# A grouped 3x3 convolution as 32x32 products on 16 tiles of the array, with its operand copies spread over five engines

## The chip, the cores and the metric

The kernel runs on one core of a Trainium2 chip. The metric is device time in microseconds (us) of one execution. A core has a matrix engine (TensorE, PE in the profile; its weight loads are shown as PEld), VectorE (DVE), ScalarE (ACT), GpSimd (POOL) and SyncE (SP), which issues transfers. Each engine keeps its own program order, and they meet at semaphores. Transfers run on 16 DMA engines. Tensors live in SBUF, 128 partitions wide; products are summed in PSUM, which has eight banks of 512 float32 numbers in each partition.

## What is computed

The input is `x`, 8 images of 128 channels and 56 x 56 pixels, float32. Four layers follow each other, each of the form `x = x + layer(group_norm(x))`, the norm being over 32 groups of four channels of one image:

- layer 0: attention between windows of 8 x 8 pixels, with a depthwise 3x3 convolution;
- layer 1: a batch norm, a projection, and a recurrence of 512 units over all pixels in order, then a projection back;
- layer 2: the layer that is changed, below;
- layer 3: two 3x3 convolutions with batch norms and a residual.

Layer 2 in the reference, with `O = I = 128` and `p = 4`:

```python
i = jnp.arange(O)[:, None]
j = jnp.arange(I)[None, :]
m3 = (j - i) % p == 0
w3m = w3 * m3[:, :, None, None].astype(w3.dtype)
out = conv_general_dilated(x, w3m, window_strides=(1, 1), padding=((1, 1), (1, 1)))
w1m = w1 * (~m3).astype(w1.dtype)
out = out + jnp.einsum('oi,bihw->bohw', w1m, x)
out = out + b.sum(axis=1)[None, :, None, None]
```

So the channels fall into four classes of 32 (by their number modulo 4). Within a class there is a 3x3 convolution of 32 x 32 channels; between different classes there is a 1x1 convolution. The kernel keeps channels sorted by class, one class in each quarter of 32 partitions.

## The kernel before

All eight images stay in SBUF as `X`, 128 partitions by 8 x 3136 pixels. An image is cut into seven blocks of 8 rows (448 pixels; `NBLK = 7`), 56 blocks in all, and a block's sum takes one PSUM bank.

**Layer 2** (in `convolutions`). `Norm` makes an image's statistics on VectorE (`bn_stats` per block, then an aggregate), spreads them over the four channels of a group with two small products on PE (`mean_mm`, `var_mm`), takes a root on ScalarE, and then writes the normalised image with a border of zeros into one of two buffers `pads` (L1314, VectorE). `spread` (L1318 to L1333) builds `g3`: for every class, its 32 channels three times, in three quarters of the partitions, moved by 0, 1 and 2 pixels. Of the twelve pieces of each chunk of rows, three are copies by ScalarE (L1331) and nine are transfers, issued by SP or by GpSimd (L1333). `within` (L1343) does a block's taps: for each of three filter rows and each class one product with 96 rows of weights and 32 columns, so that the four classes use four column tiles of the array. `between` (L1351) adds the 1x1 convolution as one 128x128 product, two blocks at a time. `add` (L1358) adds the sum and the bias to `X` on VectorE, and `stats3` (L1421) makes the statistics for layer 3.

The order of PE, ScalarE, VectorE and GpSimd is the order in which the loop over the 56 blocks writes the instructions (`manual_schedule`): in block `n` of image `b` the loop does the taps, then small steps of the next image's norm, then the adds, then the next image's `normal` and `spread`. Transfers issued by SP are in the order of the program too. Layer 2 starts when layer 1's last outputs are in `X`; before its first product, image 0 must have been normalised and spread. Products that only keep PE at work (`warm`, L897) fill that time.

**Layer 1.** The recurrence runs over 17 stretches of pixels at once, two pixels per turn of the loop. Within the second part of its turns, VectorE takes statistics (`stats`, L984, `bn_stats` over 32 pixels of 16 stretches) of image 0 as its pixels become final; the last two pieces come after the loop. The other images' statistics are made in layer 2 (L1281).

**Layer 3** starts with image 0, whose normalised rows and transforms (`normal3`, `all_sums`) are made while layer 2 does its last image. `tail` and `late` are the last images' statistics, which are finished inside layer 3. `outputs` uses three scratch tiles `s`, `d` and `w`.

## Time and profile before

| | us |
|---|---|
| median of 3 executions | 3253.57 (3253.45 to 3254.02) |
| the profiled execution | 3253.89, its span 3251.9 |
| PE busy | 3178.3 (98%) |
| VectorE busy | 2270.8 (70%) |
| ScalarE busy | 1270.3 (39%) |
| GpSimd busy | 1475.3 (45%) |
| layer 1's recurrence ends, layer 2's first product | 2640, 2653.5 |
| layer 3's first product | 2844.6 |

The profile is of one execution. A line of a group names the line of the kernel, the engine, the operation, what it writes and reads, how often, the busy time and the mean duration of one in ns, and then how long the engine was idle ahead of such instructions and what ended that. Each float32 product appears as two records of PE and two of PEld. Matmuls are pipelined, so their busy times overlap, and starts tell more than durations. Times in a timeline are from the start of the span.

### The profile page before, as it was taken

To read this page: it belongs to the slowest core of one execution; us is meant where nothing else is said; L and a number is where in the kernel's file an instruction comes from. 1 tells how busy PE (TensorE), PEld (TensorE's weight loads), DVE (VectorE), ACT (ScalarE), POOL (GpSimd) and SP (SyncE) were. 2 spreads that over 40 slices of the span, in tenths; PEclk is the share of its full clock that TensorE was granted. 3 is DMA by queue.
4 is the path that set the end of the run, shared out by engine and by line. 5 is a ranking of instruction groups with operands and counts; after the bars stand their busy time and mean duration, and the time that the engine had idled before them with its cause. 6 is when DMAs were issued, how large, how long until landed. Compare 5 with 4: busy or idle time off the path is not lost.

```text
span 3251.9 us, 104559 instructions
## 1 busy us (share of the span) xinstructions
PE 3178.3 (98%) x40784; PEld 2679.8 (82%) x40784; DVE 2270.8 (70%) x5756; ACT 1270.3 (39%) x2425; POOL 1475.3 (45%) x4147
## 2 busy tenths in 40 slices
PE   8999999999999989999999999999999999999998
PEld 5767677676766679999999999999999973399998
DVE  5888888888887866666555555555532347799998
ACT  4555555555555532221111111111111244556564
POOL 4888888888777843333222222222200036522221
PEclk8999999999999999999999999999999999999999
DMA  5555555555455421110000000000022236500001
GB/s 156 135 143 131 143 137 138 142 135 143 120 137 145 121 63 49 49 49 29 1 1 1 1 1 1 1 1 1 8 58 61 59 104 166 144 16 36 31 36 46
DMA packets 188167, 239.09 MB, mean 74 GB/s; under 512 B 42848, under 2 KB 137568, under 8 KB 187664
## 3 DMA queue, kind: packets, MB, share of 16 engines
q0 software_dynamic: 40896, 123.47, 14.0%
q1 hardware_dynamic: 130256, 101.95, 10.9%
q10 hardware_dynamic: 16512, 6.90, 0.9%
q8 instruction: 324, 5.31, 0.7%
q14 instruction: 179, 1.47, 0.2%
HBM read 133.64 MB, written 67.56 MB: 62 GB/s over the span
## 4 chain that ended last, share of the span: by engine, by line
PE 83%; DVE 10%; issue 2%; POOL 2%; ACT 1%; DMA 1%; ACTq 0%; POOLq 0%; DVEq 0%; SPq 0%
PE ps L1086 27%; PE q L1051 9%; PE po L1116 5%; PE s L539 5%; PE po L605 5%; PE pc L1343 4%; PE t L581 4%; PE plep L420 4%; PE pc3a L1663 3%; PE pc3b L1663 3%; PE pi L1021 3%; DVE nmax L546 2%; PE t L571 2%; PE pc L1351 1%; PE py L446 1%
## 5 line engine op out<-in xcount | busy, mean ns | idle before, releaser
L1086 PE MATMUL ps<-hs,w_gates 128*128 128x136 f32 x7680 | 928.8, 279 | 0.0
L1086 PEld LDWEIGHTS ps<-hs,w_gates 128*128 128x128 f32 x7680 | 911.6, 190 | 4.5
L1100 ACT ACTIVATE hs<-v 128x272 f32<-128x272 f32 x538 | 212.3, 404 | 1167.3 <-DVE v L1098 1167.3
L546 DVE TENSOR_REDUCE nmax<-s 128x2 f32<-128x512 f32 x784 | 486.3, 684 | 169.3 <-PE s L539 167.6
L591 ACT ACTIVATE e<-t 128x512 f32<-128x512 f32 x784 | 429.5, 596 | 339.8 <-PE t L581 261.8
L1098 DVE TENSOR_TENSOR v<-ps,g 128x272 f32<-128x272 f32 x538 | 216.3, 411 | 494.6 <-PE ps L1086 407.3
L1039 POOL TENSOR_TENSOR d<-inp 128x136 f32<-128x136 f32 x186 | 87.8, 472 | 789.1 <-DVE inp L1027 789.1
L498 POOL COPY ks<-kT 128x64 f32 x1568 | 297.2, 235 | 120.6 <-PE t L581 69.0
L605 PE MATMUL po<-e,ring 128*32 128x64 f32 x12544 | 244.9, 230 | 6.1 <-DVE nmax L546 5.5
L605 PEld LDWEIGHTS po<-e,ring 128*32 128x32 f32 x12544 | 217.9, 149 | 31.0 <-DVE nmax L546 7.9
L581 PE MATMUL t<-qm,ks 32*128 32x128 f32 x6272 | 237.3, 273 | 1.3 <-issue 1.3
L539 PE MATMUL s<-ks,qm 32*128 32x256 f32 x3136 | 233.9, 403 | 4.4 <-ACT vp L342 2.3
L581 PEld LDWEIGHTS t<-qm,ks 32*128 32x128 f32 x6272 | 220.1, 187 | 3.3 <-issue 2.2
L1663 PE MATMUL pc3a<-va,u_w1c_t 128*128 128x196 f32 x1152 | 198.3, 330 | 7.6 <-POOL va L1517 5.8
L1116 PE MATMUL po<-hs,xw 128*128 128x272 f32 x744 | 204.1, 397 | 0.2
L1663 PEld LDWEIGHTS pc3a<-va,u_w1c_t 128*128 128x128 f32 x1152 | 190.4, 189 | 13.6 <-POOL va L1517 11.0
L1663 PE MATMUL pc3b<-vb,u_w2c_t 128*128 128x196 f32 x1152 | 195.8, 328 | 0.0
L1663 PEld LDWEIGHTS pc3b<-vb,u_w2c_t 128*128 128x128 f32 x1152 | 191.7, 189 | 0.0
L539 PEld LDWEIGHTS s<-ks,qm 32*128 32x128 f32 x3136 | 146.6, 185 | 34.4 <-issue 4.7
L1051 PE MATMUL q<-d,mixed 128*128 128x136 f32 x1116 | 160.2, 279 | 0.5 <-DVE g L1065 0.3
L500 POOL TENSOR_TENSOR qm<-q,hmask 128x128 f32<-128x128 f32 x392 | 154.0, 393 | 0.0
L1116 PEld LDWEIGHTS po<-hs,xw 128*128 128x128 f32 x744 | 132.0, 190 | 22.1 <-ACT hs L1100 0.6
(317 smaller groups left out, 5372.3 us busy)
## 6 DMA issues: line engine op xcount, KB each, us to landing
ring<-vpix SPq DMA_DIRECT2D x1176, 32.0 KB
v<-vimg POOLq DMA_DIRECT2D x56, 290.0 KB, 4.0
v<-vimg POOLq DMA_DIRECT2D x56, 289.5 KB, 4.8
v<-vimg POOLq DMA_DIRECT2D x56, 289.0 KB, 5.7
kept<-g SPq DMA_DIRECT2D x56, 272.0 KB, 2.4
g<-kept SPq DMA_DIRECT2D x56, 272.0 KB, 2.6
xkeep<-X POOLq DMA_DIRECT2D x56, 224.0 KB, 2.7
vimg<-vrow POOLq DMA_DIRECT2D x54, 232.0 KB, 2.7
```

Source lines behind the costliest of these rows:

```text
L498: nc.gpsimd.tensor_copy(kw[:, t : t + 1, :], ks[b][:, bass.ds(at, 1), :])
L539: nc.tensor.matmul(s_["s"][g][:, o, :], w["qm"][h].rearrange("p h x -> p (h x)"), w["kw"][h], start=True, stop=True,)
L546: nc.vector.tensor_reduce(s_["nmax"][:, :, g], s_["s"][g], AX.X, ALU.max, negate=True)
L581: nc.tensor.matmul(s_["t"][g][:, o, c], w["kw"][h, c * P : (c + 1) * P], w["qm"][h].rearrange("p h x -> p (h x)"), start=False, stop=(o == ...
L591: nc.scalar.activation(s_["e"][g], s_["t"][g], AF.Exp)
L605: mm = nc.tensor.matmul(po[g * CL : (g + 1) * CL, h, o], flat[:, at : at + 8 * CL - 7 : 8], s_["e"][g][:, o, c, h * WPX : (h + 1) * WPX], ...
L1051: nc.tensor.matmul(q[n // 3][:, n % 3], w, x, start=True, stop=True)
L1086: nc.tensor.matmul(ps[f][:, i], whh[:, k, m * P : (m + 1) * P], prev[k // 2][:, (s - 1) % 2, k % 2].rearrange("p c b -> p (c b)"), start=( ...
L1098: nc.vector.tensor_tensor(v[:, i : i + n], ps[f][:, i : i + n], x, ALU.add)
L1100: nc.scalar.activation(to, x, AF.Tanh)
L1116: nc.tensor.matmul(po, wout[:, k, :], hs[k // 2][:, :, k % 2], start=(k == 0), stop=(k == KH - 1))
L1663: nc.tensor.matmul(bank[:, half].rearrange("p (y x) -> p y x", x=H4), u[:, dy, k, :], v[:, k, i * RB + dy : i * RB + dy + RB, :], start=(d ...
```

## The change

Layer 2's taps and its 1x1 convolution become products of 32 rows and 32 columns. Row group `k` (32 partitions) of the array holds two of the eight outer taps for all four classes, and for the 1x1 part the rows of its own class. The centre tap goes into the 1x1 weights (`w1` masked, plus the centre weights masked the other way). A block thus needs three steps of four products on each of four row groups, 48 products instead of 13. The row groups work on different blocks at one time: row group `k` is 5 sub-steps behind row group `k - 1` (`LAG`), and a sub-step has up to 16 products, four row groups times four classes. Up to seven sums are open, so `ps_c` has seven banks and `ps_g` one. Before a row group starts on a block, PE waits for a token: a memset of one number by GpSimd which waits for the products of three sub-steps before.

Each row group needs every class's channels in its own 32 partitions. `pads` holds the class of that number; `turned[0]`, `turned[1]` and `turned[2]` hold the next, the one after and the third after, all normalised with a border. `turned[1]` is written by ScalarE from `X`, half the partitions at a time (`swapped`). Of the eight quarters of `turned[0]` and `turned[2]` one is written by VectorE, one by ScalarE, and six are transfers from `pads`, on SP's queue (for image 0 those of `turned[2]` on GpSimd's). `turned` has one buffer, so each chunk of rows is written again as soon as a row group has left it. `pads` is written by ScalarE (by VectorE for image 0).

The statistics of all images for layer 2 are taken in layer 1, one or two at a turn of the loop, where before only image 0's were; the last two pieces of each image come at the start of layer 2. The norms of images 2 to 7 are made together. Layer 3's statistics of image 7's last four blocks, rather than those of eight blocks, are made inside layer 3. There `w` shares its memory with another scratch tile, `fg`.

The core of the diff:

```diff
-    st2 = const.tile([P, 8, 6], F32, name="st2")
+    st2 = [const.tile([P, 8, 6], F32, name="st2")]
...
+    rest2 = keep.tile([P, B - 1, 8, 6], F32, name="rest2")
+    st2 += [rest2[:, b] for b in range(B - 1)]
...
-                    stats(len(cuts) - 2 - len(done))
-                    if len(done) == 1:
-                        stats(len(cuts) - 2)
+                    spans = [len(cuts) - 2 - len(done)] + [SPANS - 3] * (len(done) == 1)
+                    known_.extend((b, j) for b in range(B) for j in spans)
                     done.pop(0)
+                for b, j in known_[: 1 if len(done) else 2]:
+                    stats(b, j)
+                del known_[: 1 if len(done) else 2]
...
-            ps_c = p2.enter_context(tc.tile_pool(name="ps_c", bufs=4, space=PSUM))
+            ps_c = p2.enter_context(tc.tile_pool(name="ps_c", bufs=7, space=PSUM))
+            turned = [padded(pool2, f"turned{j}", [P, PW, PW]) for j in range(3)]
...
+            CHUNKS = ((0, 18), (18, 34), (34, 50), (50, PW))
+            BEGIN = ((0, 10), (10, 18), *CHUNKS[1:])
...
+            def plain(b, rows, scalar=True):
+                lo, hi, x = inside(b, rows)
+                dst = pads[b % 2][:, lo:hi, 1 : 1 + HW]
+                if scalar:
+                    nc.scalar.activation(dst, x, AF.Identity, bias=of2[:, b : b + 1], scale=rs2[:, b : b + 1])
+                else:
+                    nc.vector.tensor_scalar(dst, x, gm2[:, b : b + 1], rs2[:, b : b + 1], ALU.subtract, ALU.mult)
+
+            def swapped(b, rows, h):
+                lo, hi, x = inside(b, rows)
+                to, of = slice(64 * h, 64 * h + 64), slice(64 - 64 * h, 128 - 64 * h)
+                nc.scalar.activation(
+                    turned[1][to, lo:hi, 1 : 1 + HW], x[of], AF.Identity,
+                    bias=of2[of, b : b + 1], scale=rs2[of, b : b + 1],
+                )
+
+            def shifted2(b, rows, k, direct=()):
+                lo, hi, x = inside(b, rows)
+                for j in (0, 2):
+                    c = (k + 1 + j) % 4
+                    to, of = slice(k * CL, (k + 1) * CL), slice(c * CL, (c + 1) * CL)
+                    dst = turned[j][to, lo:hi, 1 : 1 + HW]
+                    if j in direct or (k, j) == (0, 0):
+                        nc.vector.tensor_scalar(
+                            dst, x[of], gm2[of, b : b + 1], rs2[of, b : b + 1], ALU.subtract, ALU.mult
+                        )
+                    elif (k, j) == (2, 2):
+                        nc.scalar.activation(
+                            dst, x[of], AF.Identity, bias=of2[of, b : b + 1], scale=rs2[of, b : b + 1]
+                        )
+                    else:
+                        (nc.gpsimd if j and not b else nc.sync).dma_start(
+                            turned[j][to, rows[0] : rows[1], :], pads[b % 2][of, rows[0] : rows[1], :]
+                        )
...
+            RING = [(y, x) for y in range(3) for x in range(3) if (y, x) != (1, 1)]
+            ROWS, LAG, passed = 4, 5, {}
...
+            def taps(t):
+                for s in range(3 * t, 3 * t + 3):
+                    left = False
+                    for k in range(ROWS):
+                        n, part = divmod(s - LAG * k, 3)
+                        if not 0 <= n < B * NBLK:
+                            continue
+                        b, i = divmod(n, NBLK)
+                        if part == k == 0:
+                            pcs[n] = ps_c.tile([P, WS, HW], F32, name=f"pc2_{n}", tag="pc")
+                        own = slice(k * CL, (k + 1) * CL)
+                        for c in range(4):
+                            if part == 0:
+                                w, src, y, x = w1[own, c * CL : (c + 1) * CL], pads[b % 2], 1, 1
+                            else:
+                                w, (y, x) = w3[own, part - 1, c, :], RING[2 * k + part - 1]
+                                src = pads[b % 2] if c == k else turned[(c - k - 1) % 4]
+                            mm = nc.tensor.matmul(
+                                pcs[n][c * CL : (c + 1) * CL], w,
+                                src[own, i * WS + y : (i + 1) * WS + y, x : x + HW],
+                                start=(k == 0 and part == 0), stop=(k == ROWS - 1 and part == 2),
+                                skip_group_check=True,
+                            )
+                            if k and part == c == 0:
+                                after(mm, passed[s - (LAG - 2)])
+                        left = left or (part == 2 and k < ROWS - 1)
+                    if left:
+                        token = nc.gpsimd.memset(mark, 0.0)
+                        after(token, mm)
+                        passed[s] = token
...
+                starts = (0, 1, 2, 4, 6)
+                for _, n, k in sorted((3 * starts[n] + LAG * k, n, k) for n in range(5) for k in range(4)):
+                    if n > 1 or k:
+                        shifted2(0, BEGIN[n], k)
+                second.stats(1)
+                for t in range(B * NBLK + DONE[-1]):
+                    b, i = divmod(t, NBLK)
+                    taps(t)
...
+                    n = t - DONE[-1]
+                    if n >= 0:
                         add(n)
+                    if 0 < n <= LAST:
+                        stats3(*divmod(n - 1, NBLK))
+                    for to in (b, b + 1):
+                        if not 1 <= to < B:
+                            continue
+                        at = t - NBLK * (to - 1)
+                        if 2 <= at <= 5:
+                            plain(to, CHUNKS[at - 2])
+                        for rows, i0, free in zip(CHUNKS, (0, 2, 4, 6), (2, 4, 6, 6)):
+                            for h in range(2):
+                                if at == free + DONE[2 * h + 1]:
+                                    swapped(to, rows, h)
+                            if at - free in DONE:
+                                shifted2(to, rows, DONE.index(at - free))
...
-                s, d, w = (blk.tile([P, 2, RB * H4], F32, name=f"{k}_{name}", tag=k) for k in ("s", "d", "w"))
+                s, d, w = (
+                    blk.tile([P, 2, size], F32, name=f"{k}_{name}", tag=tag)[:, :, : RB * H4]
+                    for k, tag in (("s", "s"), ("d", "d"), ("w", "fg"))
+                )
...
-            tail = Rest(B - 2, B)
-            late = [(B - 2, NBLK - 1)] + [(B - 1, i) for i in range(NBLK)]
+            tail = Rest(B - 1, B)
+            late = [(B - 1, i) for i in range(3, NBLK)]
```

The loop before, for comparison, did `within(n)` for each block, `between` and `add` for two blocks after every second, `normal` of the next image at its fourth block, and `spread` of the next image's chunks at blocks 3, 4 and 6.

247 lines of the change are left out of this document (114 added, 133 removed).

## The prediction

> **What bounds the kernel now.** I read the page first, then the table by stage, then the stage's groups by shape, then its timeline. The page says that PE is busy nearly all the time; its share of the chain says where.
>
> ```profile
> span 3251.9 us, 104559 instructions
> ...
> PE 83%; DVE 10%; issue 2%; POOL 2%; ACT 1%; DMA 1%; ACTq 0%; POOLq 0%; DVEq 0%; SPq 0%
> ```
>
> ```profile
> core 0: us, PE busy (x) PEld busy (x) DVE busy (x) ACT busy (x) POOL busy (x), PEclk, DMA share, GB/s
> 2653.00:2844.00 191.00, 189.28 (x1494) 67.13 (x1494) 131.41 (x265) 95.58 (x133) 113.02 (x233) 1.00 0.62 165
> 2844.00:2930.00 86.00, 81.91 (x489) 81.06 (x490) 83.08 (x213) 47.41 (x62) 20.74 (x30) 1.00 0.04 15
> ```
>
> Layer 2 is the first row: its first product starts at 2653.5, layer 3's at 2844.6, so it takes 191 us. PE bounds it, with the other engines at 69% or less. The start of layer 3, the second row, is bound by VectorE (83 of 86 us).
>
> ```profile
> L1343 PE MATMUL pc<-g,w 96*32 96x448 f32 x1344 | 139.3, 541 | 2.0 <-DMA g<-pad 1.0 <-issue 0.9
> ...
> L1351 PE MATMUL pc<-pad,w 128*128 128x448 f32 x112 | 49.6, 564 | 0.0
> ...
> L1331 ACT COPY g<-pad 32x928 f32<-32x928 f32 x15 | 14.5, 965 | 1.1 <-ACT g L1331 0.5 <-ACT sdb L1394 0.3
> ```
>
> ```profile
> 2668.25 4.72 PE L1343 MATMUL pc<-g,w 96*32 96x448 f32 x48
> 2672.89 1.78 PE L1351 MATMUL pc<-pad,w 128*128 128x448 f32 x4
> 2674.60 1.33 PE L1343 MATMUL pc<-g,w 96*32 96x448 f32 x12
> ```
>
> Every float32 product leaves two records: 56 blocks of 12 tap products make 1344. The 48 records of two blocks go to four column tiles, so they are 12 rounds of four; taking the last record's 0.54 us off 4.72 leaves 11 rounds, 0.38 us each (0.376 between starts in the trace). Four tiles therefore run wholly beside each other. Two blocks take 2674.60 - 2668.25 = 6.35 us, 28 such pairs 177.8; the other 13 us of the stage are waits.
>
> **The change, part by part.**
>
> *Products.* The new order has 3 x 56 + 15 = 183 sub-steps; in each, 16 products of 32x32 with 448 columns, one per tile. If all 16 run beside each other, a sub-step is two rounds: 0.752 us. Nothing in this trace uses 16 tiles. From below: the 0.752. From above: were only four tiles to run at a time, 4 x 0.752 = 3.0 us. I take 0.752, since the trace shows four column tiles at full rate here and four row tiles too (layer 0, L539: 16 records in 1.15 us, four rounds), and the dispatch of 16 pairs has been seen to be quick enough:
>
> ```profile
> 600.60 1.25 PE L605 MATMUL po<-e,ring 128*32 128x64 f32 x64
> ...
> 603.59 1.15 PE L539 MATMUL s<-ks,qm 32*128 32x256 f32 x16
> ```
>
> L605 starts 64 records in about 1.02 us (1.25 less the last one's 0.23), 16 ns each with its weight load; a sub-step has 32 in 752 ns, 23.5 ns each. So the taps need 183 x 0.752 = 137.6 us from the first to the last.
>
> [...]
>
> *Start.* Before, the mean of image 0 and its root end at 2645.2 and the first chunk of L1314 at about 2646.2. After, VectorE does two 32-partition copies of that chunk (0.8 each by L1314's 504 columns), then waits for one more weight matrix (SP loads them 0.43 apart, the third at 2646.4; the second was issued at 2645.98 and used at 2648.46, so it lands within 2.5, and I take 2.2), then four 128x128 operations of 0.28. First product: about 2649.7, after which three sub-steps run to 2652.0. Then PE holds the mean of image 1, whose statistics stand in VectorE's order behind four more chunks, five quarter copies and a sum: 2649.7 + 0.7 + 1.4 + 0.74 + 0.74 + 0.68 + 0.28 + 0.74 + 0.74 + 0.68 + 1.1 (two statistics and their aggregate) = 2657.5. PE goes on at 2657.9. GpSimd issues 13 transfers of image 0 before its first token; at 0.5 each, after the chunks, they end about 2658.6, and the token is asked for at 2659.4: hidden by less than a microsecond.
>
> *The other 180 sub-steps*: 135.4 us, to 2793.3. Eight more small products for statistics break the tile mode. The row before (product of the guard, L1411) moved the next round from 2696.75 to 2697.13: 0.38 each, 3.0 together, to 2796.3.
>
> *Tokens.* One GpSimd memset per sub-step, asked for three sub-steps later, so 1.5 us after its products end less a handover of some 0.5: hidden while POOL has nothing else, as it has after image 0. A token late by more than the spare 1.0 us would hold PE by as much. The statistics that L1281 did for the images to come, 56 of 0.61, leave VectorE's order, where they cost nothing (busy 131 of 191 us): no gain.
>
> *Copies*, per image of seven blocks, 21 x 0.752 = 15.8 us. ScalarE: 4 passes over 3136 elements in 16 instructions. By L1331's groups (965 ns for 928 columns, 578 for 463), 0.83 ns an element plus 0.19: 13.5 us; with bias and scale, 784 contiguous elements take 1.041 in layer 3 (edge, L1445), 0.2 more: 16.7. Consecutive ACTIVATEs there start 0.1 earlier than durations say: 15.1. SP: 24 transfers, all on its queue, where L1333 had 15 there and 30 on POOL.
>
> ```profile
> L1333 SPq DMA_DIRECT2D g<-pad x120: 507/543/2033, 2649.4 to 2822.2; - x120
> ```
>
> ```profile
> 2738.83 11.23 SPq L1333 DMA_DIRECT2D g<-pad x14
> ```
>
> The median issue of 0.543 and 0.09 between two make 0.63, or 15.2 us an image; the second row, 14 in 11.23, makes 0.80 with one wait inside, or 19.3. So both engines stand near the 15.8, and SP over it if issues stretch. Bytes are no limit: 6 x 32 x 58 x 58 x 4 = 2.58 MB in 15.8 us is 164 GB/s, and the stage did 165. VectorE: 7 adds (L1358, 0.68), 7 statistics (L1421, 0.605) and the quarter (L1314's 952, 896 and 392 columns: 1.26 + 2 x 0.74 + 0.68), 4.8 + 4.2 + 3.4 = 12.4. Both queues keep program order, and nearly every copy waits until PE has left the rows it overwrites; behind a waiting one stand the next chunks, for which PE waits in turn. A stall reaches PE when the transfer of rows 0 to 18 for row group 1 is late; it has about 1.8 us to spare with 4 us to land. From 0 (0.63) to 7 x 3.5 = 25 (0.80): I take 4, an issue of 0.69 with part of it covered, nearer the median as half as many bursts from POOL compete.
>
> *Handover to layer 3*: 0.9 as before (last L1351 ends 2843.75). First product at 2796.3 + 4 + 0.9 = 2801.2 against 2844.6: 43.4 gained.
>
> *Statistics in layer 1.* 42 more, 35 x 0.68 and 7 x 0.28 on VectorE.
>
> ```profile
> 1743.57:1756.98 13.41, 13.41 (x107) 12.94 (x106) 8.40 (x25) 2.47 (x6) 3.75 (x8) 1.00 0.00 1
> 1756.98:1770.38 13.40, 13.40 (x106) 12.93 (x105) 7.80 (x24) 2.47 (x6) 3.73 (x8) 1.00 0.00 1
> ...
> 2531.26:2540.65 9.39, 9.39 (x74) 9.00 (x73) 3.51 (x10) 1.91 (x7) 0.00 (x0) 1.00 0.22 61
> 2540.65:2550.03 9.38, 9.38 (x73) 9.00 (x72) 2.72 (x8) 1.90 (x7) 0.00 (x0) 1.00 0.21 60
> ```
>
> The first and third stretch are pairs of recurrence steps that hold one and two of image 0's statistics at the very place; the others hold none. Same length: PE covers them. Cost 0; without cover 25.8 us.
>
> *Layer 3*: four statistics of 0.605 leave VectorE where it bounds: 0 to 2.4, I take 1.2. The shared scratch tile is written and read by VectorE alone, in its order: 0.
>
> Sum: 43.4 + 1.2 = 44.6. The profiled execution took 3253.9 (span 3251.9 and 2.0 around it), 0.3 over the median: 3253.6 - 44.6 = 3209.0.
>
> **Rivals.**
> 1. *Copies bind layer 2.* An SP issue of 0.80 or ACTIVATEs at 16.7 us an image. For: both at 95% or more. Against: the median issue. Price 10 to 25 us: 3219 to 3234.
> 2. *Sixteen tiles are not fed* (slower). PE does not run them all beside each other, or its instruction stream cannot deliver 64 instructions per sub-step (85 a microsecond; layer 0 takes 1734 in 40 us, 43). It decides where a sub-step passes 0.752 + 44.6 / 180 = 1.0 us. At two rounds of eight, 1.5: 180 x 0.75 = 135 more, 3344; at 1.1, about 3272. For: no row with 16 tiles. Against: L605's dispatch.
> 3. *Statistics are not covered in layer 1.* 25.8 back: 3235. Against: the stretches above.
>
> **Numbers.** My forecast 0.60, rival 1 0.18, rival 2 0.16 beyond 1.0 us and 0.03 short of it, rival 3 0.03. Its own range is 3198 (no copy stall, start 3 us earlier, all of layer 3's 2.4) to 3219. With rival 1 and the near cases the range is 3198 to 3248. Anything within 0.2%, 6.5 us, cannot be told from no change: faster 0.82, same 0.02, slower 0.16.
>
> **What would show it.** Tap records in rounds of 16 with starts 0.376 apart; the first at 2649 to 2651, a gap near 2652 that ends with image 1's mean; layer 3's first product near 2801; PE waiting for DMA or ACT some 4 us; layer 1's pairs still 13.41 and 9.38. Wrong if rounds are over 0.5, or SP issues are back to back with PE waiting.

## The result, and the profile after

The changed kernel takes 3260.52 us (median of 20 executions, 3255.78 to 3263.5) against 3254.91 for the kernel before (20 executions beside them): a ratio of 1.0017, with a 95% interval of 1.0010 to 1.0024. It is slower by a little, where 3209 was forecast, in a range of 3198 to 3248. The profiled execution took 3262.5 and has a span of 3260.7.

The page of the changed kernel, its span and its chain:

```profile
span 3260.7 us, 112218 instructions
...
PE 80%; DVE 13%; issue 3%; POOL 2%; ACT 1%; DMA 1%; ACTq 0%; POOLq 0%; SPq 0%; DVEq 0%
```

The table by stage, cut at the first product of layer 2 (2656.2) and of layer 3 (2852.0):

```profile
core 0: us, PE busy (x) PEld busy (x) DVE busy (x) ACT busy (x) POOL busy (x), PEclk, DMA share, GB/s
2656.20:2852.00 195.80, 189.57 (x5395) 115.43 (x5395) 120.41 (x240) 134.60 (x138) 23.31 (x191) 0.94 0.49 115
2852.00:2930.00 78.00, 76.98 (x446) 76.69 (x447) 74.27 (x188) 43.75 (x56) 17.71 (x21) 0.96 0.04 16
```

Layer 2 takes 195.8 us where it took 191.1 before. PE is "busy" for 97% of it, and no other engine for more than 69%, but this busy time counts a product from its start to its modelled end and says nothing about how many run at once. The column of the granted clock (PEclk) hints at more: it is 0.94 over the stage and 0.96 after it, where both rows of before had 1.00.

The layer's own groups, over the same stretch:

```profile
L1396 PE MATMUL pc<-pad,w 32*32 32x448 f32 x2688 | 186.3, 557 | 1.9 <-issue 1.9
L1396 PE MATMUL pc<-turned,w 32*32 32x448 f32 x2688 | 182.9, 555 | 0.5
...
L1347 ACT ACTIVATE turned<-X,of,rs 64x896 f32<-64x896 f32 x31 | 35.1, 1132 | 11.1 <-PE pc L1396 10.4
...
L1406 POOL MEMSET mark<- 1x1 f32 x168 | 16.1, 96 | 164.8 <-PE pc L1396 160.3 <-remote 3.6 <-PE pn L1466 0.8
```

The tokens (L1406) wait for PE, 160 us in all, and the copies of the ACT group wait for PE too. The waits of the layer's weight loads, from 2656 to 2852:

```profile
PEld pc L1396 <- issue: 40.8, 99, 2.5
...
PEld pc L1396 <- ACT turned L1364: 0.8, 1, 0.8
```

One of them, of 0.8 us, ends with a copy, none with a transfer or a token; "issue" means that the profile shows nothing that the load waited for. So the bound is in PE itself or in its stream of instructions, and the question is why it is slower than two rounds of 0.376 per sub-step. The same table for the middle of layer 2 gives the rate:

```profile
2690.00:2810.00 120.00, 117.77 (x3764) 76.15 (x3772) 78.03 (x142) 93.49 (x94) 11.04 (x117) 1.00 0.55 128
```

3754 of the 3764 records are taps. A full sub-step has 32, so one takes 120 x 32 / 3754 = 1.02 us, against 0.752 in the prediction and 1.0 as the point from which the change loses.

Where the 50.8 us went between the forecast of layer 3's first product (2801.2) and its real start (2852.0), read from the starts of products and tokens:

| | us |
|---|---|
| layer 0 and layer 1 end later than before | 5.1 |
| from there to the end of sub-step 23 (token at 2689.9, forecast about 2674.2) | 10.6 |
| the other 159 sub-steps | 35.1 |

### The profile page after: what moved, and what is told of

Same layout as the page of the kernel before. It is cut to its first block, busy times and chain, and to the rows that moved or that the text cites. A ratio compares the mean times of both kernels' runs of the same rounds, so it can differ in the third digit from the quotient of the medians.

```text
span 3260.7 us, 112218 instructions
## 1 busy us (share of the span) xinstructions
PE 3181.4 (98%) x44684; PEld 2730.9 (84%) x44684; DVE 2280.3 (70%) x5758; ACT 1308.0 (40%) x2427; POOL 1379.7 (42%) x4094
## 4 chain that ended last, share of the span: by engine, by line
PE 80%; DVE 13%; issue 3%; POOL 2%; ACT 1%; DMA 1%; ACTq 0%; POOLq 0%; SPq 0%; DVEq 0%
PE ps L1092 27%; PE q L1057 9%; PE pc L1396 6%; PE s L541 6%; PE po L1122 5%; PE po L607 5%; PE t L583 4%; PE plep L422 4%; PE pi L1027 3%; DVE nmax L548 2%; PE t L573 2%; PE py L448 1%; PE pvp L321 1%; PE pk L293 1%; PE pq L392 1%
## 5 line engine op out<-in xcount | busy, mean ns | idle before, releaser
L1396 PE MATMUL pc<-pad,w 32*32 32x448 f32 x2688 | 186.3, 557 | 1.9 <-issue 1.9
L1396 PE MATMUL pc<-turned,w 32*32 32x448 f32 x2688 | 182.9, 555 | 0.5
```

What stands on the lines that cost most here:

```text
L1396: mm = nc.tensor.matmul(pcs[n][c * CL : (c + 1) * CL], w, src[own, i * WS + y : (i + 1) * WS + y, x : x + HW], start=(k == 0 and part == 0 ...
```

## The experiments

The runs weigh six theories. A: PE's instructions arrive too slowly. B: PE issues in order and leaves holes; in a later form, it holds only so many unfinished products. C: the copies bind. D: the tokens bind. E: the granted clock falls at the two ends of the layer. F: the new addresses of tiles slow down layer 0. The kernel before took 3254.8 to 3257.0 beside these runs; each ratio is against its own.

### Twice the instructions for the same columns

```diff
-                            mm = nc.tensor.matmul(pcs[n][c * CL : (c + 1) * CL], w,
-                                src[own, i * WS + y : (i + 1) * WS + y, x : x + HW], ...)
+                            for half in range(2):
+                                lo, hi = half * WS // 2, (half + 1) * WS // 2
+                                mm = nc.tensor.matmul(pcs[n][c * CL : (c + 1) * CL, lo:hi], w,
+                                    src[own, i * WS + y + lo : i * WS + y + hi, x : x + HW], ...)
```

> Every 32x32 product of layer 2 is issued as two of 224 columns: the same columns and sums, twice the instructions (128 for a full sub-step). Theory A, supply of instructions: the changed kernel's PE gets 256 instructions in about 4.05 us, so a full sub-step of 64 takes 1.02 us; with 128 it takes about 2.03, and the 168 of them cost some 170 us more, about 3430. Theory B, order of issue (a first product that waits for its tile holds the next weight load for 0.187 us more): at most a second such hole per sub-step, 1.02 to about 1.2, so 3280 to 3295. Theory C, the copies bind, and theory D, the tokens bind: nothing that they do changes, 3260.

Measured: 3603.7 (one execution), far beyond every theory. The table of the stage shows why the run can't tell A from B:

```profile
2700.00:3100.00 400.00, 400.00 (x8198) 352.56 (x8182) 86.96 (x162) 101.73 (x102) 11.56 (x128) 0.50 0.19 44
```

The granted clock is 0.50 through the whole layer. 8198 records in 400 us are 3.1 us for a sub-step of 64. At a clock of 0.50 a tile's passes of 448 columns start 0.75 us apart (in the changed kernel from 2662.05 on), where they start 0.38 apart at 1.00. So, by estimate, passes of 224 columns take half of 0.75, and the four of a tile's two half products 1.5 us; this is two such times, as if only eight of the sixteen tiles worked at once. A limit on the number of unfinished instructions could do that (the two halves of one tile follow each other in the stream), but this run doesn't show it: by the count used further below it never has more than 26 weight loads unfinished, where other runs reach 33. As a test of A it is inconclusive.

### Fewer products, with the same tiles, tokens and copies

```diff
-                        for c in range(4):
+                        for c in range(2 if part else 4):
...
```

> Left out: the taps of two of the four classes, 16 of a block's 48 products, so that a full sub-step has 42.7 instructions on average in place of 64; the other two classes keep their tiles as full as before, the tokens and the copies stay. Theory A: 42.7 at 63 a us is 0.68, so the tiles' own 0.752 binds instead of 1.02; about 148 sub-steps gain up to 0.265 each, 3220. Theory B: 0.752 + 0.187 = 0.94 stays, 11 us gained, about 3249. Theories C and D: 3260.

Measured: 3237.59 (3235.1 to 3239.6), ratio 0.9943 (0.9927 to 0.9960). The tokens come 0.72 to 0.79 us apart over most of the layer, two rounds of 0.376, so neither the tokens (D) nor the work of a tile forbid the predicted sub-step. It is the number of products that makes the difference, as A and the later form of B say. The gain is less than the 35 us that a steady 0.752 would give, because now the copies hold PE:

```profile
PEld pc L1396 <- DMA turned<-pad: 8.1, 4, 3.8
```

This is the prediction's first rival, at its place and for 8 us: with PE at the predicted rate, the transfers are late now and then. In two of these waits PE stood idle for 2.4 and 2.8 us of a stretch of 3.4, and in the next 3.4 us the granted clock was 0.50. In the changed kernel itself PE is too slow to meet this rival.

### No copies

```diff
-                                src = pads[b % 2] if c == k else turned[(c - k - 1) % 4]
+                                src = pads[b % 2] if c == k or b else turned[(c - k - 1) % 4]
...
-                        for rows, i0, free in zip(CHUNKS, (0, 2, 4, 6), (2, 4, 6, 6)):
-                            for h in range(2):
-                                if at == free + DONE[2 * h + 1]:
-                                    swapped(to, rows, h)
-                            if at - free in DONE:
-                                shifted2(to, rows, DONE.index(at - free))
```

> Left out: from image 1 on, the copies of the other classes (ScalarE's, VectorE's and the transfers); every product then reads the normalised image itself, with the same shapes, instructions and tokens. Theory C: with no copies the sub-steps fall from 1.02 to 0.94 or less, 3220 to 3249. Theories A, B and D: the sub-steps stay at 1.0 to 1.02, 3255 to 3260.

Measured: 3252.95 (3249.7 to 3255.9), ratio 0.9992 (0.9983 to 1.0002). The middle of the layer, without a transfer:

```profile
2690.00:2810.00 120.00, 118.98 (x4090) 92.24 (x4086) 65.04 (x131) 26.67 (x28) 11.60 (x127) 1.00 0.03 10
```

4067 of these records are taps: 0.944 us a sub-step. So the copies cost 0.08 of the 1.02, and the larger part of the miss, 0.944 against 0.752, is there without them. The median distance of two tokens is 0.95 in both kernels; what differs is the long ones: between 2690 and 2835, 27 of 140 distances are over 1.05 us in the changed kernel, often four apart, and 9 of 149 here. Four sub-steps are 256 instructions. The DMA records of the changed kernel's trace hold 354 packets of 16,384 bytes for PE's instructions, in this layer one per 4.05 us (the median). PE and its weight loads have 89,368 records in all, so a packet holds some 250 instructions, by estimate. Here are five of the places where no weight load starts for long in the changed kernel, each a multiple of 128 loads after the one before:

```
last load   next load   instruction packet ended   from its end to the next load
2716.76     2717.68     2716.31                    1.37
2720.90     2721.98     2720.56                    1.42
2762.23     2762.95     2761.59                    1.36
2774.21     2775.13     2773.63                    1.50
2778.39     2779.43     2778.14                    1.29
```

Of the 27 pauses over 0.45 us between 2690 and 2835, 24 end 1.2 to 1.6 us after such a packet. Without the transfers there are five such pauses, and two of them do. So PE seems to wait for the next block of its program. Theory A holds, then, but for 0.08 us of the sub-step only; that it is the copies' transfers which delay the packets is inferred from these two runs.

How many such blocks PE holds ahead, no run here shows.

### The 1x1 part as one product of 128x128

```diff
+                if t < B * NBLK:
+                    pcs[t] = ps_c.tile([P, WS, HW], F32, name=f"pc2_{t}", tag="pc")
+                    nc.tensor.matmul(pcs[t], w1, pads[b % 2][:, i * WS + 1 : (i + 1) * WS + 1, 1 : 1 + HW],
+                        start=True, stop=False, skip_group_check=True)
-                for s in range(3 * t, 3 * t + 3):
+                for s in range(2 * t, 2 * t + 2):
...
-                        n, part = divmod(s - LAG * k, 3)
+                        n, part = divmod(s - LAG * k, 2)
```

> Same result by other products: the 1x1 part of a block (16 products of 32x32) is one product of 128x128 with the same weights, ahead of the block's two sub-steps of taps; the lag is 3 of the new sub-steps, two tokens a block in place of three. PE's columns stay at three times 0.752 = 2.26 us a block, the instructions fall from 192 to 132. Theory A: 132 at 63 a us are 2.09, so the columns' 2.26 binds where 3.05 are taken now; 56 blocks gain up to 43 us, about 3218. Theory B: three holes of 0.187 a block stay, 2.8, about 3248. Theory C: the copies of an image need 18 to 19 us or 2.6 to 2.7 a block, about 3240. Theory D: two tokens a block, 2.6 at best, 3240 to 3260.

Measured: 3262.01 (3260.1 to 3264.5), ratio 1.0021 (1.0012 to 1.0031): no gain, though a block has 132 instructions where it had 192. A alone is refuted. The timeline of the weight loads of one block shows the other mechanism, undisturbed:

```profile
2749.89 0.30 PEld L1383 LDWEIGHTS pc<-pad,w 128*128 128x128 f32 x2 [0.73 <-DVE X L1415]
2750.84 0.10 PEld L1398 LDWEIGHTS pc<-pad,w 32*32 32x32 f32 x1 [0.65 <-issue]
2750.85 0.12 PEld L1398 LDWEIGHTS pc<-turned,w 32*32 32x32 f32 x4
...
2751.25 0.10 PEld L1398 LDWEIGHTS pc<-pad,w 32*32 32x32 f32 x1 [0.17 <-issue]
2751.63 0.10 PEld L1398 LDWEIGHTS pc<-pad,w 32*32 32x32 f32 x1 [0.28 <-issue]
2751.82 0.18 PEld L1398 LDWEIGHTS pc<-turned,w 32*32 32x32 f32 x8
```

The 128x128 product ends at 2750.91 by the model, the last tap ahead of it at 2749.96, and all 16 products of a sub-step start within 0.1 us from 2750.84: sixteen tiles do run beside each other. At 2751.25 the second pass of the first tile starts (0.41 later), and the weights of that tile's next product, the 17th, are loaded. Its passes start at 2751.63, which is 0.38 later, as predicted. But the 18th product's load comes only at 2751.82, though its tile is free at 2751.63: that is 0.57 after the start of the first product's second pass, 0.533 for the record of that pass and 0.03 more. The 18th product waits until the first has left the array. Theory B in its first form called this a hole of 0.187 (2751.82 - 2751.63); it is the difference between the 0.57 and the 0.38 after which the tile itself is free.

The counts agree. At the start of any weight load the trace gives the number of loads started less the number of passes ended: it is never over 33 in the changed kernel, nor in the runs without copies, with half the columns and with filled row groups, and each of them reaches it. That is 16 products with both loads and the first load of the 17th; ahead of that load 32 loads and their 32 passes are unfinished, 64 instructions. With 17 products in 0.967 us (from a product's first load to the load that waits for its end), 16 take 0.91 at this limit, by estimate. The run without copies took 0.944; what makes the other 0.03 is open.

The block as a whole takes 3.13 us: the 128x128 product hardly overlaps with the taps (by less than 0.1 us of the modelled ends). Its load waits 0.73 us after the last tap's load in most blocks, whatever the profile names as the end of that wait, and the next sub-step's loads wait until the product is all but over.

### Half the columns

```diff
-                                pcs[n][c * CL : (c + 1) * CL], w,
-                                src[own, i * WS + y : (i + 1) * WS + y, x : x + HW],
+                                pcs[n][c * CL : (c + 1) * CL, : WS // 2], w,
+                                src[own, i * WS + y : i * WS + WS // 2 + y, x : x + HW],
...
```

on top of the run without copies; `add` takes the same half.

> Left out: the copies from image 1 on, as in the run without copies, and the second half of every block's columns (224 of 448; the other half of the output is not made). A full sub-step has the same 64 instructions and half the columns. Theory B, now with numbers: PE keeps at most 64 instructions, 16 products of two passes, unfinished; the run without copies shows a product from its weight load to the next load that waits for its end at 0.967 us (0.40 between its passes, 0.533 for the second, 0.03). With 224 columns that is about 0.59, and 16 of 17 of it 0.56 a sub-step. Theory A: 256 instructions come no faster than one block per 3.5 to 4.05 us, so a sub-step stays at 0.87 or more. Both can hold, A then being the larger: 0.87 to 1.0.

Measured: 3232.16 (one execution). The tokens' median distance is 0.578 us, near theory B's 0.56; the mean is 0.90, since at nearly every 128th load PE pauses for 1.2 to 2.0 us, until 1.2 to 1.6 after an instruction packet's end. The packets come 3.58 us apart. Both mechanisms fit, each with its own size: at most 17 unfinished products, and for a sub-step of 64 instructions, by estimate from the packets, no less than about 0.9 us (3.58 / 4) with quiet DMA queues (a share of 0.03) and about 1.0 (4.05 / 4) with the copies (0.55).

### Products of 64 rows for the 1x1 part

```diff
+                            two = slice(pair * 2 * CL, (pair + 1) * 2 * CL)
+                            for c in range(4):
+                                mm = nc.tensor.matmul(
+                                    pcs[n][c * CL : (c + 1) * CL], w1[two, c * CL : (c + 1) * CL],
+                                    pads[b % 2][two, i * WS + 1 : (i + 1) * WS + 1, 1 : 1 + HW],
+                                    start=not pair, stop=False, skip_group_check=True,
+                                )
...
-                            if part == 0:
-                                w, src, y, x = w1[own, c * CL : (c + 1) * CL], pads[b % 2], 1, 1
-                            else:
-                                w, (y, x) = w3[own, part - 1, c, :], RING[2 * k + part - 1]
-                                src = pads[b % 2] if c == k else turned[(c - k - 1) % 4]
+                            w, (y, x) = w3[own, part, c, :], RING[2 * k + part]
+                            src = pads[b % 2] if c == k else turned[(c - k - 1) % 4]
```

> Same result: the 1x1 part of a block becomes eight products of 64 rows and 32 columns (row groups 0 and 1 together, then 2 and 3 together) in place of sixteen of 32x32; a block has 40 products and 160 instructions instead of 48 and 192, the tiles are as full as before, the taps and the copies are the same, the row groups follow each other after 4, 3 and 4 sub-steps. A sub-step has 13.3 products on average. Theory B: 13.3 of 17 in 0.967 is 0.76, so the tiles' 0.752 nearly holds; theory A: 53 instructions at 63 a us are 0.84. Both: 0.80 to 0.84 where 1.02 were, 26 to 32 us less, 3229 to 3235. If instead every sub-step with a waiting product has the 0.187 hole whatever the number of instructions: 0.94, 3249. If the copies bind from 0.85 on: about 3240.

Measured: 3463.96 (3463.8 to 3468.6), ratio 1.0643 (1.0629 to 1.0658). No theory had this. The loads of PE:

```profile
2751.27 0.22 PEld L1394 LDWEIGHTS pc<-pad,w 64*32 64x32 f32 x8 [1.45 <-issue]
2752.94 0.13 PEld L1410 LDWEIGHTS pc<-turned,w 32*32 32x32 f32 x2 [1.45 <-issue]
...
2754.76 0.20 PEld L1394 LDWEIGHTS pc<-pad,w 64*32 64x32 f32 x8 [1.45 <-issue]
```

Products of 64 rows and of 32 rows do not overlap here, although they use different row groups: at each change of the tile's shape shown, no load starts for 1.45 us, twice or more per block. The granted clock, which fell to 0.50 at the layer's start, is 0.50 from 2670 on through the layer, and at that clock the changed kernel's passes start 0.75 us apart in place of 0.38. From 2700 to 3000 PE has 3486 records, 11.6 a us, where the changed kernel has 31.4 in the middle of its layer. So shapes that alternate cost more here than the instructions saved; how much of the 200 us is the order and how much the clock, this run doesn't separate.

### Fourteen products in place of sixteen

```diff
-                        for c in range(4):
+                        for c in range(2 if k == ROWS - 1 else 4):
...
```

on top of the run without copies.

> Left out: the copies from image 1 on, as in the run without copies, and row group 3's products for two of the four classes, so that a full sub-step has 14 products in place of 16, each tile as full as before. Theory B, the limit of unfinished products: 17 products per 0.967 us make 14 in 0.80, where the run without copies takes 0.94 for 16. If the hole of 0.187 comes whenever a product waits for its tile, however many are unfinished: 0.94 again. Theory A: 56 instructions at 256 per 3.57 us, 0.78, below both. The tiles' own two rounds: 0.752.

Measured: 3233.76 (one execution). The tokens' median distance is 0.78, the mean 0.83. Between 2690 and 2810 no two loads in a row start 183 to 190 ns apart, where the run without copies has 192 such pairs. With 14 products in a sub-step the 18th product falls 1.2 sub-steps behind the first, the count of unfinished loads stays at 31 or less, and the wait for the first product's end is gone. So the rule of a hole for every waiting product (0.94) is refuted, and what a limit on unfinished products says is confirmed: the hole goes when the count stays below 33. The 0.78 itself can't tell the limit's 0.80 from theory A's 0.78.

### Idle row groups filled

```diff
+                    for k, lo, hi in ((1, 0, LAG), (2, 0, 2 * LAG), (0, 168 + LAG, 999), (1, 168 + 2 * LAG, 999)):
+                        if lo <= s < hi and s < 168 + 3 * LAG:
...
+                            for c in range(4):
+                                nc.tensor.matmul(
+                                    idle[k, lo][c * CL : (c + 1) * CL], w1[own, c * CL : (c + 1) * CL],
+                                    X[own, 0 if lo else B - 1, :BLK].rearrange("p (u v) -> p u v", v=HW),
+                                    start=True, stop=True, skip_group_check=True,
+                                )
...
-                    if t == 0:
+                    if t == 1:
                         second.mean_mm()
```

> The changed kernel with 32x32 products into unused banks (160 of them, their sums are read by nobody) on row groups that have nothing to do yet at the start or no more at the end of layer 2, so that 12 to 16 tiles are at work from the first sub-step to the last, and with image 1's mean one block later in PE's order. Theory E, the granted clock: the profile of the changed kernel shows 0.50 from 2660 to about 2676 and 0.50 to 0.75 from 2850 to 2860, with 4 to 8 of 16 tiles at work; filled, the clock stays at 1.0 and 10 to 14 us go: 3246 to 3250. If the start is held by the copies of image 0 instead: 3257 to 3260.

Measured: 3257.58 (3253.3 to 3261.5), ratio 1.0009 (1.0000 to 1.0019). The changed kernel at the start and at the end of the layer, then this run after it had waited at the start:

```profile
2659.50:2676.50 17.00, 14.97 (x158) 5.60 (x168) 8.93 (x27) 8.52 (x11) 4.24 (x13) 0.50 0.56 155
2843.80:2847.20 3.40, 3.40 (x42) 1.36 (x44) 1.84 (x6) 0.27 (x1) 0.09 (x1) 1.00 0.02 5
2847.30:2857.40 10.10, 9.22 (x41) 6.13 (x34) 6.75 (x20) 1.38 (x3) 0.60 (x6) 0.50 0.00 0
```

```profile
2663.80:2677.40 13.60, 13.60 (x197) 6.33 (x201) 6.09 (x19) 3.95 (x5) 0.53 (x6) 0.50 0.41 118
```

At the end of the changed kernel's layer the clock falls to 0.50 with PE busy all through the 3.4 us ahead, but with only eight tiles at work and then four; layer 3's first products still run at 0.50, until 2857.5. At the start it falls after three sub-steps of four tiles, and PE also stands idle there for 2.9 us, from 2658.6, before image 1's mean, so that place alone can't tell the two reasons apart. Filling cured the end (the clock is 1.00 from 2677.4 on, and layer 3 takes 407.9 in place of 408.7), but not the start. There PE stood idle for 2.6 us of a stretch of 3.4, the clock fell at 2663.8, and it stayed at 0.50 for 13.7 us although 12 tiles were at work again. What PE waited for:

```profile
2656.94 6.10 POOL L1368 DMA_DIRECT2D turned<-pad  x12 [4.64 <-DVE pad L1341]
2663.03 0.09 POOL L1417 MEMSET mark<- 1x1 f32 x1
```

PE's next product waited from 2660.1 to 2663.2 for the token at 2663.03, which stands behind GpSimd's twelve transfers of image 0.

### The statistics alone

The kernel before with the layer 1 part of the change (images 1 to 6):

```diff
-    st2 = const.tile([P, 8, 6], F32, name="st2")
+    st2 = [const.tile([P, 8, 6], F32, name="st2")]
+    rest2 = keep.tile([P, B - 2, 8, 6], F32, name="rest2")
...
+                    known_.extend((b, j) for b in range(B - 1) for j in spans)
...
```

To make room, two small tiles of layer 2 (`m1`, `bmat`) share a slot, and its tile `st` for statistics has one buffer.

> One part of the change alone: the kernel before, with the statistics of images 1 to 6 taken in layer 1 (image 7's stay where they were for want of memory) and layer 2's products as before. If the statistics cost nothing in layer 1, as predicted, 3253 to 3256, the same as before. In the profile of the changed kernel layer 0, which the change does not touch, is 4.8 us longer: if that comes with the statistics' memory, which lies ahead of other tiles, it is 3258 to 3261 here, and layer 0 is longer by as much. If layer 1's vector work shows: later by up to 20.

Measured: 3260.79 (3259.6 to 3263.0), ratio 1.0015 (1.0006 to 1.0024). In layer 1 the statistics do cost nothing here, and 0.35 us at one place (2451.6) in the changed kernel. The changed kernel's turns, at the places of those shown of before:

```profile
1748.33:1761.74 13.41, 13.41 (x107) 12.94 (x106) 8.41 (x26) 2.48 (x6) 3.74 (x8) 1.00 0.00 1
1761.74:1775.14 13.40, 13.40 (x106) 12.93 (x105) 8.41 (x26) 2.47 (x6) 3.74 (x8) 1.00 0.00 1
```

But this part alone makes the kernel as slow as the whole change does. Layer 0, which it does not touch, is longer by 4.7 us: the instructions that both profiles share start later by 4.2 at 150 us, by 6.0 at 1080 and by 4.72 all through layer 1 (in the changed kernel by 3.8, 6.0 and 4.76). The profile of this run has another 3.8 us in layer 2 (194.9 against 191.1). Its granted clock was 0.50 there for two stretches of 3.4 us, from 2658.6 and from 2784.9, where the kernel before had 1.00 all through; at half the clock they can be worth up to half of these 6.8 us, 3.4, by estimate.

### The statistics' tile at the other end of SBUF

```diff
-    rest2 = keep.tile([P, B - 1, 8, 6], F32, name="rest2")
+    right = ctx.enter_context(tc.tile_pool(name="right", bufs=1, side="right"))
+    rest2 = right.tile([P, B - 1, 8, 6], F32, name="rest2")
```

> The changed kernel with one difference: the tile that holds the statistics of images 1 to 7 lies at the other end of SBUF, so that the tiles of layer 0 and layer 1 have the addresses that they have in the kernel before. Theory F, addresses: the changed kernel and the run with the statistics alone both lose 4.7 us in layer 0, whose instructions are the same; with the old addresses layer 0 is as long as before and the whole 4.7 us shorter, 3255 to 3256. If it comes from the program (other instruction blocks) and not from the addresses: 3260.

Measured: 3254.69 (3250.5 to 3261.3), ratio 0.9998 (0.9989 to 1.0007): 5.8 us less than the changed kernel, from which it differs by the place of one tile alone. But layer 0 is not as long as before again, as theory F had it: of the 7.4 us between the two profiles' spans 2.3 lie in layers 0 and 1, 4.3 in layer 2, whose instructions are the same, and 0.8 in layer 3. Why layer 2 was shorter is open. The product that writes layer 1's output, first and last start, in the kernel before, the changed kernel, the statistics alone, this run and the next one:

```profile
L1116 PE MATMUL po<-hs,xw x744: 392/392/498, 1520.3 to 2640.2; 128*128 128x272 f32 x186
```

```profile
L1122 PE MATMUL po<-hs,xw x744: 392/392/497, 1525.0 to 2645.3; 128*128 128x272 f32 x186
```

```profile
L1122 PE MATMUL po<-hs,xw x744: 392/392/497, 1525.0 to 2644.9; 128*128 128x272 f32 x186
```

```profile
L1123 PE MATMUL po<-hs,xw x744: 392/392/497, 1522.7 to 2643.0; 128*128 128x272 f32 x186
```

```profile
L1123 PE MATMUL po<-hs,xw x744: 392/392/498, 1520.6 to 2640.9; 128*128 128x272 f32 x186
```

4.7 us late with the tile ahead of the others, twice; 2.4 and 0.3 late with it at the other end. The other traces agree: in all ten kernels with the tile ahead this first start lies from 1523.9 to 1526.0, and in the three with it at the other end at 1520.6, 1522.3 and 1522.7. Layer 0 differs by 1 or 2 us from run to run at its start, but between 120 and 1080 us the changed kernel falls back by 2.6 us, the last two of these by 0.0 and 0.9. What in layer 0 depends on the address is open.

### The version that is faster than both

On top of the filled row groups, the tile at the other end and image 0's copies between the sub-steps:

```diff
-                for _, n, k in sorted((3 * starts[n] + LAG * k, n, k) for n in range(5) for k in range(4)):
-                    if n > 1 or k:
-                        shifted2(0, BEGIN[n], k)
+                firsts = sorted((3 * starts[n] + LAG * k, n, k) for n in range(5) for k in range(4) if n > 1 or k)
+                def image0(until):
+                    while firsts and firsts[0][0] < until:
+                        _, n, k = firsts.pop(0)
+                        shifted2(0, BEGIN[n], k)
+                image0(9)
...
                     taps(t)
+                    image0(3 * t + 12)
```

> The run with filled row groups, with two more differences: the statistics' tile at the other end of SBUF, and image 0's copies issued in the order of need between the sub-steps, so that GpSimd's first token no longer stands behind twelve transfers (it came at 2663.0 in the filled run, where PE had waited for it since 2660.1). Theory F: 4.7 us less than the filled run's 3257.6. Theory E with the token freed: 3 us for the wait, and up to 6 more if the clock then stays at 1.0 from 2660 to 2676: 3244 to 3250. If the copies of image 0 then arrive later and bind: 3253.

Measured: 3243.77 (3240.1 to 3247.9), ratio 0.9964 (0.9951 to 0.9978): faster than the kernel before by 0.36%, and just past the best that was expected. GpSimd's queue and the clock:

```profile
2652.83 0.99 POOL L1369 DMA_DIRECT2D turned<-pad  x2 [4.63 <-DVE pad L1342]
2654.32 0.44 POOL L1418 MEMSET mark<- 1x1 f32 x1 [0.50 <-PE pc L1397]
```

```profile
2651.80:2832.00 180.20, 177.60 (x5636) 119.17 (x5635) 120.47 (x240) 134.77 (x138) 24.02 (x188) 1.00 0.53 125
2660.00:2675.00 15.00, 15.00 (x456) 10.10 (x470) 10.67 (x26) 9.78 (x11) 5.39 (x22) 1.00 0.73 190
```

The first token comes at 2654.3, the clock stays at 1.00, and layer 2 takes 180.2 us against 195.8. Of the 21.0 us between the two profiles' spans 4.4 lie in layers 0 and 1, 15.6 in layer 2 and 1.0 in layer 3. The middle of the layer is nearly as slow as ever, 0.998 us a sub-step.

### A shorter lag

```diff
-            ROWS, LAG, passed = 4, 5, {}
+            ROWS, LAG, passed = 4, 4, {}
```

> The fastest version so far (statistics' tile at the other end, filled row groups, image 0's copies in order of need) with a lag of 4 sub-steps between row groups in place of 5: three sub-steps fewer from the first to the last, 2.9 us, if the tokens are not late: 3240 to 3242. A token is asked for two sub-steps after its products were issued, 1.9 us; products end 0.93 after their start and the token takes some 0.4, so 0.5 are spare. If every token is late by 0.1 or more, 16 us and more are lost: 3255 and up.

Measured: 3244.97 (3243.5 to 3245.8), ratio 0.9962 (0.9949 to 0.9976): the same as with a lag of 5. The expected 2.9 us did not come; the sub-steps in the middle take 1.022 on average where they took 0.998, some 4 us in all. Late tokens are the smaller part of that: the weight loads wait for one in three places, 0.9 us in all. The pauses over 0.25 us that end 1.2 to 1.65 us after an instruction packet take 3.5 us more than in the run with a lag of 5, between 2690 and 2810 alone. Why there are more of them is open.

## Why the prediction was wrong, point by point

- **Products: the term that failed.** "If all 16 run beside each other, a sub-step is two rounds: 0.752 us." All 16 do run beside each other, but a product is unfinished for 0.967 us, so a lasting 0.752 would have 16 x 0.967 / 0.752 = 21 products unfinished at once, by estimate. No count here found PE with more than 17. The row that the forecast was taken from, with four tiles, has no more than 12 weight loads unfinished and never meets the limit. The limit gives 0.91, by estimate; measured without copies: 0.944. At 159 sub-steps that is 159 x 0.192 = 30.5 us.
- **The stream of instructions**, named in the second rival ("cannot deliver 64 instructions per sub-step") and set aside on the strength of 64 records in 1.02 us: that row is a burst, and this limit is one of blocks of 256, which came 4.05 us apart. Measured: 0.08 a sub-step while the copies run, about 13 us. Together with the first term the sub-step is 1.02, just past the 1.0 at which the rival said that the change turns slower. The two make some 43 us; the forecast had allowed 4 for the copies and 3 for small products in the same stretch, and that leaves about the 35.1 of the table. The rival was right in kind and was given too small a chance.
- **Sixteen tiles against one.** The forecast took 16 times the rate of one tile. Without copies, 0.752 x 16 / 0.944 = 12.7x was measured, with copies 11.8x. The 1.1 us at which the second rival has 3272 is an estimate that no run shows; the sub-step took 0.944 and 1.02.
- **Start.** The first product was forecast for 2649.7 and came at 2656.2; 5.1 of that is layers 0 and 1. The pause for image 1's mean ended at 2662.05 in place of 2657.9. Then two things cost more than was allowed for. GpSimd's first token, "hidden by less than a microsecond", came at 2663.3 behind its transfers. And the clock of 0.50, which no step had, ran from 2659.5 to 2676.6. 10.6 us in all; the fastest version, with image 1's mean later, the token freed and the clock held, has its layer 2 15.6 us shorter.
- **Copies.** 4 us of stall were allowed; PE's waits show 0.8. They are there once PE is faster (8.1 us in the run with two classes), so the step was sized for a PE that didn't come. What the copies do cost in the changed kernel is the 0.08 above, as it seems through the instruction packets.
- **Statistics in layer 1.** Cost 0 there, right but for 0.35 us: 13.41 and 13.40 again. Wrong is what the step left out, the tile that they need: with it ahead of the others, layer 0 was 4.7 us longer.
- **Small products and handover**: the 3.0 and 0.9 are consistent with the trace (last tap's end 2851.1, layer 3 at 2852.0), the first not measured by itself.
- **Layer 3.** Forecast 1.2 shorter, measured 408.7 against 407.3: 1.4 longer, with the clock at 0.50 in its first 5.5 us. With the clock held it takes 407.7.
- **The sum**: 5.1 + 10.6 + 35.1 + 2.6 = 53.4 more than forecast, on 3209.0, makes 3262.4; the profiled execution took 3262.5. The low end of the forecast's own range is mis-added: no copy stall, 3 us at the start and 1.2 in layer 3 make 3200.8, not 3198.

## What to carry to other kernels

A rate seen with few tiles need not be the rate with many: here a round of passes took 0.376 us with four tiles and 0.472 (half of 0.944) with 16. Work out how many products must be unfinished at once for every tile to find its next one waiting (the time that one is unfinished, 0.967 us here, times the rate), and compare with the most that any row shows (12 weight loads with four tiles, 33 with 16). This stream of short products had two further prices that the burst of 64 records in 1.02 us did not show: blocks of 256 instructions that came too late, for 0.08 us a sub-step while the copies ran, and a granted clock of 0.50 after PE had been idle for 2.4 to 2.8 us of a stretch of 3.4, or had had only eight and then four tiles at work in one. Keep tiles of one shape together (a change of shape cost a wait of 1.45 us at a clock of 0.50) and the idle row groups busy (with them filled the clock was 1.00 at the layer's end). When memory is added ahead of other tiles, look at stages that the change does not touch (layer 0 was 4.7 us longer), by comparing the starts of the same instructions in both traces.

## What was not expected of the hardware

- Seventeen float32 products, the last with one of its two weight loads, are the most that were unfinished in any count (33 loads); the 18th waited for the end of the first, 0.19 us past the time at which its tile was free.
- Products of 32x32 overlapped with 128x128 by less than 0.1 us of the modelled ends, and not with 64x32 even on different row groups, where no load started for 1.45 us at a change (at a clock of 0.50).
- The granted clock fell to 0.50 with PE busy but only eight and then four of 16 tiles at work, at the end of the changed kernel's layer 2, as it did after PE had been idle for 2.4 to 2.8 us of 3.4. With 12 to 16 tiles at work from the start and the token on time it was 1.00 through the 180.2 us of the layer; once fallen, it stayed at 0.50 for 13.7 us with 12 at work, and through the rest of the layer in two of the runs.
- One tile of 1344 bytes in each partition (1152 in one kernel), put ahead of others, went with a layer of 1100 us that was 3.6 to 5.7 us longer in ten programs; in the three where it lay at the other end, it was 0.3 to 2.4 longer.
